# Gate projections in their inputs' banks, attention sums and statistics in the halves of the silu group, and q's projection one half later, in a linear-attention and Mamba kernel

## The chip, the cores and the metric

The kernel runs on one core of one Trainium2 chip. The metric is the device time of a run in microseconds (us), lower is better. The engines are called PE (TensorE), DVE (VectorE), ACT (ScalarE), POOL (GpSimd) and SP (SyncE, which issues all the DMAs here). PSUM is the small memory that PE writes to, in banks of 128 partitions by 512 floats.

## The reference

The input x has shape (8, 512, 48, 48): 8 samples, 512 channels, L = 2304 positions, all in float32. Two layers follow each other, each with a group norm ahead (32 groups of 16 channels) and a residual sum behind it.

```python
# layer 0: causal linear attention, 8 heads of 64
xn = group_norm(x)
q, k = elu(Wq xn) + 1, elu(Wk xn) + 1;  v = Wv xn
S_t = S_(t-1) + k_t v_t^T                       # 64 x 64 per head
out_t = (q_t S_t) / (q_t . cumsum(k)_t + 1e-10)
x = x + out
# layer 1: four Mamba blocks, 128 channels each; each gets the one before added to its input
x_i = group_norm(x)[block i] (+ fused of block i-1)
xp, z = in_proj(x_i);  xs = silu(conv4(xp) + b)  # 256 channels each, 4 causal taps
dt, B, C = x_proj(xs); delta = softplus(dt_proj(dt) + b)
h_t = exp(delta_t A) h_(t-1) + delta_t xs_t B_t  # 16 states per channel
y = (sum_n C_t h_t + xs D) * silu(z);  x_m = out_proj(y)
fused = sigmoid(mean x_i) x_i + sigmoid(mean max(x_i, x_m)) max(x_i, x_m)
x = x + concat(fused)
```

## The kernel before

The whole program is one stream of instructions per engine, in an order that Python code writes out by hand (a manual schedule). Nothing is reordered afterwards: each engine executes its instructions in the order in which they were issued, and waits where one of them needs the result or the buffer of another engine.

**Jobs, slots and halves.** A Mamba block of one sample is cut into six chunks of LC = 384 positions. One chunk is a *job*; there are 8 x 4 x 6 = 192, of two streams (even and odd samples) in turns. A job has 8 *slots*: two halves of the channels by four groups of states. A slot has four scans, so each job has 32 (`scan`, L830, one DVE instruction of 128 x 385). For every scan ACT computes a *decay* (`decay`, L819, an exp into a PSUM bank). DVE makes most of the scan's other input for the next slot at the top of each slot (`product`, L809), POOL the rest of it (`last_product`, L798). POOL multiplies the results with C (`weigh`, L846), PE adds them up in the bank `yp` (`gather`, L853, two slots later), and DVE multiplies by silu(z) (`gated`, L865). `finale` then projects the output (`project`, L871, PE) and takes the maximum (L882, DVE).

All other work is put between the scans. A slot is two *halves*: `beside(2k)` is called after the product and ahead of the first two scans of slot k, `beside(2k + 1)` ahead of the last two. So a job has 16 halves; below they are numbered 0 to 15 within the job that is being scanned, half 0 being its first. Everything else is written as Python generators (tasks) that yield `(when, banks)`: they go on when `when` is due, which is a number of halves since their last stage ("1"), a half (an int), or a half and a gap (a pair), and when so many PSUM banks are free. Attention chunks are kept in the list `heads`, other work in `tasks`; in each half the stages of heads that need no bank are issued first, then tasks and heads in order.

**Banks.** Six PSUM banks, in the list `spare`, are shared by the decays and by every other task. `take` takes the first free one, and `free` puts it back at the end as soon as its last reader has been issued; whoever takes it next waits on the chip for that reader. `ahead(n)` issues decays until n of them are ready or no bank is free: DEPTH = 3 after every scan, DEPTH + 2 before the silu and softplus groups.

**Preparing a job** (`prepare`) is done while the job before it is scanned. The convolutions are matmuls with scaled weights (`conv`, L635), `gate` (L646) is z's projection. Then comes the silu group on ACT (L670 to L675: a table load, four silus; the next decay loads the exp table again), x's projection (L681), a copy to `dbc` (L686), dt's projection (L694), the softplus group (L705, again with a table load ahead and one behind), and the transfers of delta, B and C by SP. In most jobs the silu group is issued in half 14 and the softplus group in half 2. ACT's work on the residual stream (`pass_on`: fu L596, xi L597, xb L601 or L607) is issued in half 2 too, ahead of it.

**Attention** (`chunk`) goes by chunks of 384 positions and 128 channels (two heads), 192 in all. `times[m]` is the half at which chunk m starts; in the steady state it is 3 within the job, so that its stage `at(j)` is issued in half 3 + j of that job or of the next one. The stages: q's projection (`project(0)`, L288, four k-tiles), its features (`feature`: exp L300 and relu L301 on ACT, then min and add on DVE, L345), the same for k (L353) and v (L359), running sums of k (L364, L374), transposes (L381), denominators and products of k and v in one bank called `both` (L393, L398), their sums into S (L401 to L410, DVE), the reciprocal spread over the head (`rdb` L414, transposed into `rb`, L418), the scaled q (L423, DVE), scores (L431), mask (L436), output (L445, L449), residual and statistics (L452, L454). After a block's last chunk `group_norm` computes the norm of layer 1 in five stages (L169 to L195). `statistics` reads the next samples in 24 pieces each for layer 0's norm (L242).

Of the kernel before, what the change touches and what calls it, by code (L numbers as in the profile page):

```python
# [16 lines left out]
P = 128  # L17
# [32 lines left out]
def attention_then_mamba_kernel(  # L50
# [111 lines left out]
    def group_norm(stats, n, name, bufs):  # L162
# [3 lines left out]
        yield "1", 1  # L166
# [5 lines left out]
        yield "1", 0  # L172
# [11 lines left out]
        yield "0", 1  # L184
        var_ps = bank()
        nc.tensor.matmul(var_ps[:, 0:n], grp, gm[:, 2, :], start=True, stop=True)
        yield "1", 0
# [4 lines left out]
        yield "1", 0  # L192
# [16 lines left out]
    def statistics(b):  # L209

        xv = x[b].rearrange("(t p) l -> p t l", p=P)
        stats = small.tile([P, 4, NC, 6], F32, tag="stats_a", name=f"stats_a{b}", bufs=1)
# [20 lines left out]
        else:  # L233
            for ct in range(4):
                for c in range(NC):
                    yield "2", 0
                    if (ct, c) == (0, 0):
                        nxt = piece(b, 0)
                    xs = nxt
                    i = ct * NC + c + 1  # L240
                    nxt = piece(b, i) if i < 4 * NC else None
                    nc.vector.bn_stats(stats[:, ct, c, :], xs)  # L242
# [25 lines left out]
    def chunk(m):  # L268
# [54 lines left out]
        yield at(0), 1  # L323
# [17 lines left out]
        yield at(1), 0  # L341
        ex = feature(qp, qb)
        yield at(2), 0
        q = new("q", 2)
        nc.vector.scalar_tensor_tensor(q, ex, 1.0, qp, ALU.min, ALU.add)  # L345
        bank.free()
        yield at(2, 0), 1
        kp, kb = project(1)
        yield at(3), 0
        ex = feature(kp, kb)  # L350
        yield at(4), 0
        k = new("k", 2)
# [15 lines left out]
        if ksum is not None:  # L368
            kept = new("kept")
            nc.scalar.copy(kept[64:128], kc[64:128])  # L370
            save(ksum[:, cols], kept[64:128])
# [17 lines left out]
        yield at(12), 1  # L389
# [9 lines left out]
        yield at(14), 0  # L399
# [11 lines left out]
        bank.free()  # L411
        yield at(15), 0
        rdb = new("rdb", 1, (P, 2 * NT, 64))
        nc.scalar.copy(rdb, rd.unsqueeze(2).to_broadcast([P, 2 * NT, 64]))  # L414
        yield at(16), 1
        rb = bank()[:, 0:LC].rearrange("p (i t) -> p i t", i=NT)
# [4 lines left out]
        yield at(18), 0  # L421
# [34 lines left out]
        if c + 1 == NC:  # L456
            norm = yield from group_norm(stats, 1, f"m{b}_{o}", 8)
            flush()
            done[b, o] = norm
# [156 lines left out]
    class Job:  # L616
# [6 lines left out]
        def prepare(self):  # L623
# [20 lines left out]
            def gate(h):  # L644
                zp = bank()[:, 0:LC]
# [7 lines left out]
                return zp  # L653
# [5 lines left out]
            yield "1", 1  # L659
            xc0 = conv(0)  # L660
            yield "2", 2
            xc1 = conv(1)
            zp0 = gate(0)
            yield "1", 0
# [6 lines left out]
            bank.free()  # L671
            zp1 = gate(1)
            nc.scalar.activation(xs[:, 1, :], xc1, AF.Silu, bias=pv[:, 1:2])
            nc.scalar.activation(sz[0], zp0, AF.Silu)
            nc.scalar.activation(sz[1], zp1, AF.Silu)  # L675
            converting.clear()
            bank.free(3, late=True)
            yield "1", 1
# [513 lines left out]
```

## Time and profile before

| | |
|---|---|
| runs (median, lowest to highest) | 9334.64 us (9323.44 to 9344.09), 3 runs |
| the profiled execution | 9323.3 us, its span 9321.5 us |
| granted TensorE clock | 0.948 |
| busy: DVE, POOL, PE, ACT | 8348.4, 8080.8, 7735.1, 6580.2 us |
| scans L830 | 6144, 5475.1 us, 938 ns each |
| decays L819 | 6144, 3431.3 us, 579 ns each |
| table loads | 382 ahead of L819, 192 each ahead of L670 and L705, 1283 ns each |
| DMA | 1642.84 MB, 176 GB/s |

A row of the profile gives the line in the kernel, the engine, the operation, the tile that it writes and those that it reads, the count, the busy time and the mean of one, then the idle time of the engine just before these instructions and who ended it. In the waits, "A <- B: us, times, longest" means that engine and line A stood idle until B. In the timeline a row has its start and its duration, both in us from the span's start, and in brackets the idle time before it. Rows of like instructions that follow each other on one engine are merged ("x3"); neighbours on DVE and ACT overlap by some 0.08 us, so that two rows can start closer together than one lasts.

### The profile page before, as it was taken

What the parts mean: (1) busy time and instruction counts of PE and PEld (TensorE: products, weight loads), DVE (VectorE), ACT (ScalarE), POOL (GpSimd) and SP (SyncE); (2) the same over time, 40 slices, a digit from 0 to 9 for tenths busy, and PEclk for the clock granted to TensorE, in tenths of its full rate; (3) what the DMA queues carried; (4) which work ended last, traced back from release to release, by engine and by line L of the source; (5) the groups of instructions that cost most, each with busy time, mean ns of one, the idle gap of its engine ahead of it and who ended that gap; (6) DMA issues with size and microseconds to landing.
All of it is one profiled execution on the core that took longest, in us unless ns stands there. A gap on an engine that the chain in (4) does not pass through costs nothing.

```text
span 9321.5 us, 120629 instructions
## 1 busy us (share of the span) xinstructions
PE 7735.1 (83%) x35714; PEld 3673.0 (39%) x35714; DVE 8348.4 (90%) x11640; ACT 6580.2 (71%) x12656; POOL 8080.8 (87%) x5635
## 2 busy tenths in 40 slices
PE   7888888888888888888888888888888888888865
PEld 4444444433344444443343444443333434444321
DVE  3899999999999999999999999999999999999997
ACT  3677777777777777777777777776777777777775
POOL 2788888889988898889998888888998888888998
PEclk9999999999999999999999999999999999999977
DMA  6566666667666666666766666667666666666654
GB/s 189 158 169 173 175 174 168 180 189 198 188 169 176 177 179 172 176 183 189 196 182 178 174 175 173 174 170 194 192 184 182 176 176 172 173 171 175 167 153 129
DMA packets 1002899, 1642.84 MB, mean 176 GB/s; under 512 B 138592, under 2 KB 797312, under 8 KB 1002240
## 3 DMA queue, kind: packets, MB, share of 16 engines
q1 hardware_dynamic: 1002240, 1635.13, 64.1%
q8 instruction: 283, 4.64, 0.2%
q14 instruction: 376, 3.08, 0.1%
HBM read 1309.06 MB, written 325.58 MB: 175 GB/s over the span
## 4 chain that ended last, share of the span: by engine, by line
DVE 39%; ACT 20%; PE 18%; issue 7%; DMA 7%; POOL 6%; SPq 2%; DVEq 0%; POOLq 0%; ACTq 0%
DVE u L830 23%; DVE u L809 8%; PE bank L288 7%; ACT bank L819 6%; PE bank L635 4%; POOL u L846 4%; ACT L819 3%; PE yp L853 3%; PE bank L646 2%; ACT L705 2%; DMA B<-scr 2%; DMA C<-scr 1%; ACT bank L301 1%; ACT delta L705 1%; DVE sm L436 1%
## 5 line engine op out<-in xcount | busy, mean ns | idle before, releaser
L830 DVE TENSOR_TENSOR_SCAN u<-bank,u 128x385 f32<-128x385 f32 (+1 forms) x6144 | 5475.1, 938 | 530.5 <-ACT bank L819 503.2
L846 POOL TENSOR_TENSOR u<-u,C 128x1536 f32<-128x1536 f32 x1536 | 4885.1, 3180 | 219.5 <-DVE u L830 112.6
L819 ACT ACTIVATE bank<-dr,av 128x385 f32<-128x385 f32 (+1 forms) x6144 | 3431.3, 579 | 1556.9 <-DVE u L830 1113.3
L853 PE MATMUL yp<-u,cst 128*64 128x384 f32 x12288 | 2429.9, 514 | 282.7 <-ACT yp L787 146.3
L798 POOL TENSOR_TENSOR u<-B,dxr 128x512 f32<-128x512 f32 x1536 | 1959.9, 1276 | 22.4 <-DMA dxr<-xscr 19.0
L288 PE MATMUL bank<-xn,wq_sb 128*128 128x384 f32 x4608 | 1855.1, 552 | 48.8 <-DVE u L830 31.7
L809 DVE TENSOR_TENSOR u<-B,dxp 128x1024 f32<-128x1024 f32 x1536 | 1834.7, 1195 | 10.7 <-ACT dxp L782 10.7
L853 PEld LDWEIGHTS yp<-u,cst 128*64 128x64 f32 x12288 | 788.3, 139 | 1476.6 <-issue 903.5
L635 PE MATMUL bank<-xi,wk 128*128 128x384 f32 x3072 | 1118.2, 507 | 280.1 <-ACT kl L385 172.7
L288 PEld LDWEIGHTS bank<-xn,wq_sb 128*128 128x128 f32 x4608 | 929.1, 212 | 862.9 <-issue 215.1
L635 PEld LDWEIGHTS bank<-xi,wk 128*128 128x128 f32 x3072 | 563.7, 193 | 862.2 <-ACT kl L385 254.1
L844 POOL COPY state<-u 128x4 f32<-128x4 f32 x1280 | 243.8, 190 | 740.6 <-DVE u L830 738.0
L300 ACT ACTIVATE ex<-bank,bqkv_sb 128x384 f32<-128x384 f32 x384 | 221.3, 576 | 561.6 <-PE bank L288 539.2
L787 ACT ACTIVATE yp<-xs,pv 128x384 f32<-128x384 f32 x384 | 223.4, 582 | 405.7 <-DVE yz L865 405.7
L819 ACT ACT_TABLE_LOAD x382 | 490.1, 1283 | 6.7
L746 POOL TENSOR_TENSOR delta<-delta,xs 128x384 f32<-128x384 f32 x384 | 385.8, 1005 | 95.5 <-DMA dscr<-delta 84.3
L418 PE MATMUL bank<-cst,rdb 128*128 128x128 f32 x576 | 112.7, 310 | 426.1 <-DVE u L830 334.7
L694 PE MATMUL bank<-dbc,wd 9*128 9x384 f32 x768 | 316.3, 524 | 65.1 <-ACT dbc L686 29.0
L646 PE MATMUL bank<-xi,wi 128*128 128x384 f32 x768 | 297.8, 500 | 59.8 <-ACT xs L670 59.8
L871 PE MATMUL bank<-yz,wo 128*128 128x384 f32 x768 | 297.6, 509 | 34.1 <-DVE yz L865 19.4
L449 PE MATMUL bank<-sm,v 128*64 128x128 f32 x2304 | 257.2, 301 | 42.4 <-DVE u L830 40.6
L418 PEld LDWEIGHTS bank<-cst,rdb 128*128 128x128 f32 x576 | 66.8, 153 | 558.9 <-ACT xb L601 272.5
(109 smaller groups left out, 7860.3 us busy)
## 6 DMA issues: line engine op xcount, KB each, us to landing
B<-scr SPq DMA_DIRECT2D x1536, 192.0 KB
C<-scr SPq DMA_DIRECT2D x1536, 192.0 KB
xn<-xn SPq DMA_DIRECT2D x192, 768.0 KB
dr<-dscr SPq DMA_DIRECT2D x768, 192.0 KB
dxr<-xscr SPq DMA_DIRECT2D x768, 192.0 KB
dscr<-delta SPq DMA_DIRECT2D x192, 384.0 KB
xscr<-delta SPq DMA_DIRECT2D x192, 384.0 KB
xn<-in_x SPq DMA_DIRECT2D x48, 768.0 KB
```

Of the source, the lines that this page charges most:

```text
L288: nc.tensor.matmul(ps, wq_sb[:, kt, j * 512 + o * P : j * 512 + (o + 1) * P], xn[:, kt, :], start=(kt == 0), stop=(kt == 3),)
L635: nc.tensor.matmul(xc, wk[:, k, h * P : (h + 1) * P], xi[:, c0 + k : c0 + k + LC], start=(k == 0), stop=(k == 3),)
L646: nc.tensor.matmul(zp, wi[:, 256 + h * P : 256 + (h + 1) * P], xi[:, c0 + 3 : c0 + 3 + LC], start=True, stop=True,)
L694: nc.tensor.matmul(vp, wd[32:41, h * P : (h + 1) * P], dbc[32:41, :], start=True, stop=True)
L746: nc.gpsimd.tensor_tensor(delta[:, h, :], delta[:, h, :], xs[:, h, :], ALU.mult)
L798: nc.gpsimd.tensor_tensor(u[:, :, :, 1 + LC - TAIL :], self.B[s % 4][:, :, cols].unsqueeze(2).to_broadcast(shape), self.dxr[s // 4][:, :, ...
L809: nc.vector.tensor_mul(u[:, :, :, 1 : 1 + LC - TAIL], self.B[s % 4][:, :, cols].unsqueeze(2).to_broadcast(shape), self.dxp.unsqueeze(1).to ...
L819: nc.scalar.activation(dA[:, cols], self.dr[h][:, g, cols], AF.Exp, scale=self.w[6][:, 2 * h + g, q + j : q + j + 1],)
L830: nc.vector.tensor_tensor_scan(u[:, j, g, cols], dA[:, cols], u[:, j, g, cols], 0.0, ALU.mult, ALU.add,)
L846: nc.gpsimd.tensor_tensor(h, h, self.C[s % 4].unsqueeze(2).to_broadcast([P, NG, 2, LC]), ALU.mult)
L853: nc.tensor.matmul(self.yp[g * 64 : g * 64 + 64, 0:LC], pair_sum, u[:, j, g, 1:], start=False, stop=(s % 4 == 3 and j == NG - 1), skip_gro ...
L871: nc.tensor.matmul(self.xm[:, 0:LC], self.w[2][:, h, :], self.yz[:, h, :], start=(h == 0), stop=(h == 1),)
```

## The change

- `prepare`: the stages of the convolutions and of the silu group get fixed halves, 12, 14 and 15. `gate` no longer takes banks: z's two projections are written into the banks of the two convolutions, each after the silu that reads it. x's projection is issued in the same half as the silu group.
- `chunk`: q's projection with the fetch of the next chunk and the load of `before` moves from `at(0)` to `at(1)`, that is from half 3 to half 4, where the output's projection (L871) is issued ahead of it. q's features move to `at(2)`, and q's min and add to `at(3)`, after k's projection. Denominators and products move from `at(12)` to `at(11)` (half 14), their sums from `at(14)` to `at(13)` (half 0), `rdb` to half 1, `rb` to half 2, the scaled q to half 3. `rb` is written into `both`, which is freed only after it. `kept` shares the buffer of `before`.
- `statistics`: for samples 2 to 7 one piece is loaded per job, two halves ahead, and its statistics are taken in half 15 (even samples) or 0 (odd ones), over 24 jobs; before it was one piece every two halves.
- `group_norm`: the five stages for layer 1 get halves of their own, 13, 14, 0, 1 and 2.

```diff
--- before.py
+++ after.py
@@ -159,17 +159,17 @@
             _, o, i = stores.pop(0)
             nc.sync.dma_start(out=o, in_=i)
 
-    def group_norm(stats, n, name, bufs):
+    def group_norm(stats, n, name, bufs, places=("1", "1", "0", "1", "1")):
 
 
         bank = Banks()
-        yield "1", 1
+        yield places[0], 1
         mv = small.tile([P, n, 2], F32, tag=f"mv{n}", name=f"mv_{name}", bufs=1)
         for ct in range(n):
             nc.vector.bn_aggr(mv[:, ct, :], stats[:, ct].rearrange("p c s -> p (c s)"))
         mean_ps = bank()
         nc.tensor.matmul(mean_ps[:, 0:n], grp, mv[:, :, 0], start=True, stop=True)
-        yield "1", 0
+        yield places[1], 0
         gm = small.tile([P, 3, n], F32, tag=f"gm{n}", name=f"gm_{name}", bufs=1)
         nc.vector.tensor_copy(gm[:, 0, :], mean_ps[:, 0:n])
         nc.vector.tensor_sub(gm[:, 1, :], mv[:, :, 0], mean_ps[:, 0:n])
@@ -181,15 +181,15 @@
         else:
             nc.vector.tensor_mul(gm[:, 2, :], gm[:, 1, :], gm[:, 1, :])
             nc.vector.tensor_add(gm[:, 2, :], gm[:, 2, :], mv[:, :, 1])
-        yield "0", 1
+        yield places[2], 1
         var_ps = bank()
         nc.tensor.matmul(var_ps[:, 0:n], grp, gm[:, 2, :], start=True, stop=True)
-        yield "1", 0
+        yield places[3], 0
         nc.vector.tensor_scalar_add(gm[:, 2, :], var_ps[:, 0:n], 1e-5)
         bank.free()
         norm = small.tile([P, 3, n], F32, tag=f"norm{n}", name=f"norm_{name}", bufs=bufs)
         nc.gpsimd.tensor_tensor(norm[:, 0, :], gm[:, 2, :], power[:, 0:n], ALU.pow)
-        yield "1", 0
+        yield places[4], 0
         for i, factor in ((0, -1.0), (1, float(L))):
             for ct in range(n):
                 nc.vector.tensor_scalar(
@@ -209,7 +209,7 @@
     def statistics(b):
 
         xv = x[b].rearrange("(t p) l -> p t l", p=P)
-        stats = small.tile([P, 4, NC, 6], F32, tag="stats_a", name=f"stats_a{b}", bufs=1)
+        stats = small.tile([P, 4, NC, 6], F32, tag="stats_a", name=f"stats_a{b}", bufs=2)
         if b == 0:
 
             xs = []
@@ -231,15 +231,13 @@
             for o in range(1, 4):
                 load_projections(o)
         else:
-            for ct in range(4):
-                for c in range(NC):
-                    yield "2", 0
-                    if (ct, c) == (0, 0):
-                        nxt = piece(b, 0)
-                    xs = nxt
-                    i = ct * NC + c + 1
-                    nxt = piece(b, i) if i < 4 * NC else None
-                    nc.vector.bn_stats(stats[:, ct, c, :], xs)
+            when = begins[b] + b % 2
+            for i in range(4 * NC):
+                yield (when - 2, 1) if b > 1 else "1", 0
+                xs = piece(b, i)
+                yield (when, 1) if b > 1 else "1", 0
+                nc.vector.bn_stats(stats[:, i // NC, i % NC, :], xs)
+                when += PERIOD
         norms[b] = yield from group_norm(stats, 4, f"a{b}", 2)
 
     def piece(b, i):
@@ -320,7 +318,7 @@
             save(xns[b].rearrange("(t p) l -> p t l", p=P)[:, :, cols], xn)
         while read[0] < m - 1:
             yield "1w", 0
-        yield at(0), 1
+        yield at(1), 1
         if o:
             xn = fetched.pop(m)
         if c == 0:
@@ -338,18 +336,16 @@
             for h in heads_of:
                 nc.sync.dma_start(out=before[h], in_=passes[b, o - 1][2][:, cols])
         qp, qb = project(0)
-        yield at(1), 0
+        yield at(2), 0
         ex = feature(qp, qb)
-        yield at(2), 0
-        q = new("q", 2)
-        nc.vector.scalar_tensor_tensor(q, ex, 1.0, qp, ALU.min, ALU.add)
-        bank.free()
         yield at(2, 0), 1
         kp, kb = project(1)
         yield at(3), 0
+        q, k = new("q", 2), new("k", 2)
+        nc.vector.scalar_tensor_tensor(q, ex, 1.0, qp, ALU.min, ALU.add)
+        bank.free()
         ex = feature(kp, kb)
         yield at(4), 0
-        k = new("k", 2)
         nc.vector.scalar_tensor_tensor(k, ex, 1.0, kp, ALU.min, ALU.add)
         bank.free()
         yield at(4, 0), 1
@@ -366,7 +362,7 @@
             nc.tensor.matmul(kc, ident, before, start=False, stop=True)
         yield at(8), 0
         if ksum is not None:
-            kept = new("kept")
+            kept = new("before")
             nc.scalar.copy(kept[64:128], kc[64:128])
             save(ksum[:, cols], kept[64:128])
         yield at(9), 0
@@ -386,7 +382,7 @@
         nc.scalar.copy(v, turned[1])
         bank.free(2)
 
-        yield at(12), 1
+        yield at(11), 1
         both = bank()
         den = both[:, 0 : 2 * NT]
         for i in range(NT):
@@ -396,7 +392,7 @@
         for i in range(more):
             for h in heads_of:
                 nc.tensor.matmul(ds[h, i, :], kl[:, i, h], v[:, i, h], start=True, stop=True)
-        yield at(14), 0
+        yield at(13), 0
         rd = small.tile([P, 2 * NT], F32, tag="rd", name=f"rd_{n}", bufs=1)
         nc.vector.tensor_scalar_add(rd, den, 1e-10)
         nc.vector.reciprocal(rd, rd)
@@ -408,17 +404,17 @@
                 nc.vector.tensor_copy(S[:, place[1], :], ds[:, 0, :])
             else:
                 nc.vector.tensor_add(S[:, place[i + 1], :], S[:, place[i], :], ds[:, i, :])
-        bank.free()
-        yield at(15), 0
+        yield at(14), 0
         rdb = new("rdb", 1, (P, 2 * NT, 64))
         nc.scalar.copy(rdb, rd.unsqueeze(2).to_broadcast([P, 2 * NT, 64]))
-        yield at(16), 1
-        rb = bank()[:, 0:LC].rearrange("p (i t) -> p i t", i=NT)
+        yield at(15), 0
+
+        rb = both[:, 0:LC].rearrange("p (i t) -> p i t", i=NT)
         for i in range(NT):
             nc.tensor.transpose(
                 rb[:, i, :], rdb[:, 2 * i : 2 * i + 2, :].rearrange("p e d -> p (e d)"), ident
             )
-        yield at(18), 0
+        yield at(16), 0
 
         nc.vector.tensor_mul(q, q, rb.rearrange("p i t -> p (i t)"))
         bank.free()
@@ -454,7 +450,9 @@
         nc.vector.bn_stats(stats[:, 0, c, :], xr)
         save(x1s[b][tile_rows, cols], xr)
         if c + 1 == NC:
-            norm = yield from group_norm(stats, 1, f"m{b}_{o}", 8)
+            norm = yield from group_norm(
+                stats, 1, f"m{b}_{o}", 8, [(times[m] + j, 1) for j in (26, 27, 29, 30, 31)]
+            )
             flush()
             done[b, o] = norm
 
@@ -641,8 +639,7 @@
                     )
                 return xc
 
-            def gate(h):
-                zp = bank()[:, 0:LC]
+            def gate(h, zp):
                 nc.tensor.matmul(
                     zp,
                     wi[:, 256 + h * P : 256 + (h + 1) * P],
@@ -650,32 +647,31 @@
                     start=True,
                     stop=True,
                 )
-                return zp
 
 
             while converting or not st.scaled:
                 yield "1w", 0
             converting.append(n)
-            yield "1", 1
+            first = 2 * self.start
+            yield (first - 20, 1), 1
             xc0 = conv(0)
-            yield "2", 2
+            yield (first - 18, 2), 1
             xc1 = conv(1)
-            zp0 = gate(0)
-            yield "1", 0
+            yield (first - 17, 1), 0
             xs = self.xs = mpool.tile([P, 2, LC], F32, tag="xs", name=f"xs_{n}")
             sz = self.sz = [
                 mpool.tile([P, LC], F32, tag="sz", name=f"sz_{n}_{h}", bufs=5) for h in range(2)
             ]
             ahead(DEPTH + 2)
             nc.scalar.activation(xs[:, 0, :], xc0, AF.Silu, bias=pv[:, 0:1])
-            bank.free()
-            zp1 = gate(1)
+
+            gate(0, xc0)
             nc.scalar.activation(xs[:, 1, :], xc1, AF.Silu, bias=pv[:, 1:2])
-            nc.scalar.activation(sz[0], zp0, AF.Silu)
-            nc.scalar.activation(sz[1], zp1, AF.Silu)
+            gate(1, xc1)
+            nc.scalar.activation(sz[0], xc0, AF.Silu)
+            nc.scalar.activation(sz[1], xc1, AF.Silu)
             converting.clear()
-            bank.free(3, late=True)
-            yield "1", 1
+            bank.free(2, late=True)
             dps = bank()
             for h in range(2):
                 nc.tensor.matmul(
@@ -744,7 +740,6 @@
             for h in range(2):
                 yield "1", 0
                 nc.gpsimd.tensor_tensor(delta[:, h, :], delta[:, h, :], xs[:, h, :], ALU.mult)
-            first = 2 * self.start
             yield "2", 0
             xsrc = spread("xscr")
             spreading.clear()
@@ -962,12 +957,17 @@
         if job.c == NC - 1:
             yield from job.stream.pass_on()
 
+
     begun, put, counted = 0, 0, list(range(1, B))
+    begins = {}
+    for b in counted:
+        first = times[parts.index((b, 0, 0))]
+        begins[b] = (first - 20) // PERIOD * PERIOD - 4 * NC * PERIOD - 1 if b > 1 else first - 64
 
     def begin(latest):
 
         nonlocal begun, put
-        while counted and times[parts.index((counted[0], 0, 0))] - 64 <= half_no[0]:
+        while counted and begins[counted[0]] - 4 <= half_no[0]:
             tasks.append(Task(statistics(counted.pop(0))))
         while put < len(parts) and times[put] - 6 <= half_no[0]:
             put += 1
```

## The prediction

> **What bounds the kernel now.** I read the busy shares on the page first, then the waits, then one pass of 16 halves in the timeline, engine by engine.
>
> ```profile
> PE 7735.1 (83%) x35714; PEld 3673.0 (39%) x35714; DVE 8348.4 (90%) x11640; ACT 6580.2 (71%) x12656; POOL 8080.8 (87%) x5635
> ```
>
> VectorE (DVE) is busy 8348.4 of 9321.5 us. The change removes no VectorE instruction, so its idle 973 us are what can be won, and new idle time there is what can be lost. The table of waits says who ends that idle time (total us, times, longest):
>
> ```profile
> DVE u L830 <- ACT bank L819: 503.2, 194, 4.7
> PE bank L418 <- DVE u L830: 334.7, 149, 2.8
> DVE q L345 <- ACT bank L301: 141.5, 63, 6.6
> DVE k L353 <- ACT bank L301: 70.8, 144, 2.3
> ```
>
> The scan waits for its decay (ScalarE, L819) once in each of the 192 jobs, 2.6 us on average. The other two VectorE waits are for q's and k's features. The timeline shows where the first lies (start, us, engine and line), in the job whose half 0 starts at 4972.03:
>
> ```profile
> 5010.54 1.19 DVE L809 TENSOR_TENSOR u<-B,dxp 128x1024 f32<-128x1024 f32 x1
> 5011.65 2.64 DVE L830 TENSOR_TENSOR_SCAN u<-bank,u 128x384 f32<-128x384 f32 x3
> 5017.47 0.96 DVE L830 TENSOR_TENSOR_SCAN u<-bank,u 128x384 f32<-128x384 f32 x1 [3.17 <-ACT bank L819]
> 5018.34 1.20 DVE L809 TENSOR_TENSOR u<-B,dxp 128x1024 f32<-128x1024 f32 x1
> ```
> ```profile
> 5011.04 1.10 ACT L819 ACTIVATE bank<-dr,av 128x384 f32<-128x384 f32 x2
> 5012.16 1.28 ACT L670 ACT_TABLE_LOAD   x1
> 5015.05 0.49 ACT L675 ACTIVATE sz<-bank 128x384 f32<-128x384 f32 x1 [0.15 <-PE bank L646]
> 5015.56 1.28 ACT L819 ACT_TABLE_LOAD   x1
> 5016.85 1.09 ACT L819 ACTIVATE bank<-dr,av 128x384 f32<-128x384 f32 x2
> ```
>
> Half 14 starts at 5010.54. The silu group (two table loads, four silus) holds ScalarE from 5012.16 to 5016.84, 4.68 us. Three decays were ahead; VectorE runs their three scans and stands 3.17 us. The next product (L809), 1.11 us of ready work, comes after the stalled scan in program order. Of these waits 159 lie in half 15 and 31 in half 0, the latter in jobs whose weights came late, so that their silu group was already issued in half 15; these are 2.4 us.
>
> The softplus group of half 2 is as heavy (1.28 + 0.87 + 1.28), yet costs nothing now:
>
> ```profile
> 4978.67 0.56 ACT L819 ACTIVATE bank<-dr,av 128x384 f32<-128x384 f32 x1
> 4979.25 1.28 ACT L705 ACT_TABLE_LOAD   x1
> 4981.43 1.28 ACT L819 ACT_TABLE_LOAD   x1
> ```
> ```profile
> 4978.57 3.49 DVE L830 TENSOR_TENSOR_SCAN u<-bank,u 128x384 f32<-128x384 f32 x4
> 4981.98 1.19 DVE L809 TENSOR_TENSOR u<-B,dxp 128x1024 f32<-128x1024 f32 x1
> ```
>
> Four scans run on without a gap, because the decay at 4978.67, a fourth one ahead, found a free bank. Lastly TensorE around half 4, which starts at 4981.98:
>
> ```profile
> 4979.66 0.52 PE L418 MATMUL bank<-cst,rdb 128*128 128x128 f32 x3 [2.32 <-DVE u L830]
> 4980.42 2.85 PE L288 MATMUL bank<-xn,wq_sb 128*128 128x384 f32 x8 [0.24 <-DVE u L830]
> 4983.10 1.50 PE L871 MATMUL bank<-yz,wo 128*128 128x384 f32 x4
> 4986.50 1.51 PE L853 MATMUL yp<-u,cst 128*64 128x384 f32 x8 [1.90 <-ACT yp L787]
> 4987.94 2.85 PE L288 MATMUL bank<-xn,wq_sb 128*128 128x384 f32 x8
> ```
>
> q's projection (first L288) fills TensorE while it would otherwise wait for yz; then the output's (L871), a gather (L853), k's projection.
>
> **What the skill says.** The Trainium skill, "ScalarE: Activation LUTs", section What ACT_TABLE_LOAD costs, gives about 1283 ns for a load plus 1380 ns of drain. The trace has the 1283 ns, but the work before ended 0.02 us ahead of the load at 4979.25: no drain shows, and I price a switch at 1.28 us. "PSUM — Partial Sum Buffer", section Terms, says that TensorE writing and another engine reading one bank at once is an error. So a gate projection into its input's bank has to wait for the silu that reads it; the trace has this wait already for the second gate (L646 after xs L670: 196.5 us, TensorE and its loads together). "Perfetto Trace Analysis", section Optimization Strategy, says that a gap that keeps repeating on the engine to be saturated can mean too few buffers. The 3.17 us gap agrees: three of the six shared banks hold convolutions and gate, so only three decays fit.
>
> **The change, part by part**, in us per job; "pitch" is from start to start.
>
> *Silu group one half later, sums and statistics moved.* At half 15 three decays are again ahead: the gates free one bank, but `both` is now taken in half 14 and holds it. From the end of the last scan of half 14, ScalarE needs a decay 0.6, the group 4.68 and a decay 0.58: 5.86. VectorE has two scans 1.74, the product 1.11, the sums (0.13 + 0.19 + three of 0.21, with gaps 0.95), 0.4 as the mean of a bn_stats (0.54, in three jobs of four), a scan 0.87: 5.07. Leaves 0.8. The late-weight jobs bear it out from the other side: 2.4 measured with the group in half 15, less 1.35 of moved work, is 1.05. To that comes the gates' turn-taking: the first gate waits for the first silu (0.58), runs 0.7, and sz follows; the second the same. At least 0.5. If TensorE also has den, S's products and a gather ahead (convolution 2.85 + 1.35 + 1.5 from about 5010.8: done 5016.6, the first silu at 5015.95), 1.15. I take a stall of 1.8, from 1.3 to 2.2. Against about 3.0 in 118 ordinary jobs that is −1.2, −142; the late-weight ones give −0.3 each, −9; the 30 with a norm at the end (now 1.3) nothing. Sum **−150**, from −260 to −60.
>
> *`both` held through rb.* This removes rb's own bank and its 2.32 us wait on TensorE. That is worth nothing directly, since q's projection has to wait for L871 anyway. But the bank is held from half 14 to half 3, where before it was free from 1 to 3. In half 2 it stands with two softplus inputs and three decays: six, and the fourth decay does not fit. Then from the start of half 2, ScalarE needs 0.1 + 0.57 (third decay, whose bank the last scan has just freed), fu 0.51, xi 0.51, mostly xb 0.6, table 1.29, softplus 0.89, table 1.30, decay 0.59: 6.36 with xb, 5.76 without. VectorE has product 1.11, two scans 1.71, the moved q product (L423) 0.46, a scan 0.87: 4.15. A new stall of 2.2 or 1.6, less the 0.35 that some jobs now lose in half 4. About +1.8 in 150 jobs: **+270**, from +60 (if fu and xi get out of the way) to +330.
>
> *q one half later.* With X the start of half 4: yz ends at X+1.66, L871 0.96 later as now, q 2.85, gather 1.44, k 2.85: k's projection ends at X+9.76 where now it ends at X+8.81. Exp and Relu add 1.03: k can be read at X+10.8. VectorE comes to L353 after half 4 (3.29), half 5 without L423 and L345 (3.10 − 0.91), half 6 with q's (1.11 + 0.46 + 1.71): X+8.76. The stall is 2.05 against 0.60 in this job: +1.45 in 177 jobs (those with their chunk at the usual place), **+257**, from +90 to +400. q's own is read after X+5.47+1.03 = 6.5, and VectorE is at 6.6: its 141.5 us shrink to about 20, **−121**.
>
> *The rest.* The norm's waits (L188, 29.4 us, for L186) get a half of their own in places: −15, from −29 to +30. The statistics' loads keep two halves of lead, at most +15.4 again (L242 for its DMA). The transfers of q's stage (fetch, `before`) leave SP one half later and are used by half 10 or in the next job; SP's B and C rows stand next to them, and 96 KB more beside 1635 MB over the span cost nothing while there are 6 halves of cover. The sharing of `kept` with `before` waits for a store 7 halves old. GpSimd (87%) gets no new work, and its waits follow VectorE's.
>
> Sum: −150 + 270 + 257 − 121 − 15 = **+241** on the span of 9321.5. The profiled run took 9323.3, so 9564 beside it; the median of the runs is 9334.6, 11 more, so 9575 beside the median, which I give.
>
> **Rivals.** (1) Faster: the stall behind silu is covered and neither new wait bites. One mechanism, k's features: if TensorE has L871 and q done early enough (k's projection done by X+7.7) and a fourth bank is there for softplus, the sum is −150 − 121 − 15 = −286: 9050. It decides below 1.5 us per job for both waits together (286 / 190). For it: stalls behind ScalarE are the largest idle item. Against: L871 can't start before yz, and 2.85 + 1.44 + 2.85 behind it are in order. (2) Only one of the two waits bites: −286 + 270 or + 257, about −20: 9315, no change within the measurement (0.2%, some 19 us, is about what a measurement of this kernel can tell). (3) Worse: gates and held banks put whole stages off by halves (needs of two banks in halves 1, 6 and 12 are met exactly), and the silu stall stays: 400 to 600 more, 9800. (4) The change doesn't do what it says: if `both` were full later than half 14, silu could have four decays ahead, and 0.87 × 150 = 130 come off my sum: 9455; I count it to mine.
>
> **Numbers.** My case 0.60 (own range 9430 to 9730), rival 1 0.15, rival 2 0.18 (a third on each side), rival 3 0.07. Faster 0.15 + 0.06 = 0.21, same 0.07, slower 0.72. The range of 8 in 10 leaves out most of rivals 1 and 3: 9190 to 9730.
>
> **What would show it.** Right: a new idle of 1.5 to 2.3 us before the fourth scan of half 3, ended by L819; L353's waits for L301 near 340 us in place of 70.8; L345's under 40; L418's wait for L830 gone; the scan's stall of half 15 gone and one of 1.3 to 2.2 in half 0; VectorE's busy time as before. Wrong: four scans without a gap after L705's table load, or k's second L288 ending before X+8.8, or L830's wait for L819 under 400 us.

## The result: 7.0% slower, and the profile after

The changed kernel takes 9982.33 us (median of 4 runs, 9981.9 to 9982.99), against 9329.04 us of the kernel before in the same runs: ratio 1.0698, 95% interval 1.0679 to 1.0716. The profiled execution has a span of 9980.4 us, 658.9 more than before, and a granted TensorE clock of 0.887 (0.948 before). Lines of the kernel have moved a little: the scan is L825 now, the decay L814, the output's projection L866, the projections of q, k and v L286, Exp and Relu L298 and L299, q's and k's min and add L345 and L349; each experiment moves them a little again, so that the scan is L823 to L830 below.

From the page, first the busy times, then the rows of the scan and of the output's projection, each before and after (busy us, mean ns of one; then the idle time before it and its releaser):

```profile
PE 8143.0 (82%) x35714; PEld 3880.4 (39%) x35714; DVE 8381.2 (84%) x11640; ACT 6601.9 (66%) x12656; POOL 8093.0 (81%) x5635
L830 DVE TENSOR_TENSOR_SCAN u<-bank,u 128x385 f32<-128x385 f32 (+1 forms) x6144 | 5475.1, 938 | 530.5 <-ACT bank L819 503.2
L825 DVE TENSOR_TENSOR_SCAN u<-bank,u 128x385 f32<-128x385 f32 (+1 forms) x6144 | 5497.0, 941 | 666.5 <-ACT bank L814 660.9
L871 PE MATMUL bank<-yz,wo 128*128 128x384 f32 x768 | 297.6, 509 | 34.1 <-DVE yz L865 19.4
L866 PE MATMUL bank<-yz,wo 128*128 128x384 f32 x768 | 518.9, 771 | 879.1 <-DVE yz L860 751.9
```

VectorE has the same work (8381.2 us, 33 more); the loss is idle time. TensorE has the same matmuls, but the output's projection takes 771 ns for each of its matmuls where it took 509. The table of waits:

```profile
DVE u L825 <- ACT bank L814: 660.9, 364, 4.3
DVE q L345 <- ACT bank L299: 365.7, 188, 5.6
DVE k L349 <- ACT bank L299: 351.7, 189, 2.0
PE bank L866 <- DVE yz L860: 751.9, 187, 4.8
```

The scan now waits for its decay 364 times, twice per job, and q's and k's features are late in nearly every job, not in 63 and 144 of 192. TensorE's wait for yz is new. One job shows how these follow each other. VectorE, from half 3 to half 7:

```profile
3285.26 0.53 DVE L419 TENSOR_TENSOR q<-q,bank 128x384 f32<-128x384 f32 x1
3285.71 0.95 DVE L825 TENSOR_TENSOR_SCAN u<-bank,u 128x385 f32<-128x385 f32 x1
3289.00 0.96 DVE L825 TENSOR_TENSOR_SCAN u<-bank,u 128x385 f32<-128x385 f32 x1 [2.34 <-ACT bank L814]
...
3290.98 0.55 DVE L860 TENSOR_TENSOR yz<-yp,sz 128x384 f32<-128x384 f32 x1
...
3298.64 0.55 DVE L345 SCALAR_TENSOR_TENSOR q<-ex,bank 128x384 f32<-128x384 f32 x1 [1.97 <-ACT bank L299]
...
3302.86 0.55 DVE L349 SCALAR_TENSOR_TENSOR k<-ex,bank 128x384 f32<-128x384 f32 x1 [1.95 <-ACT bank L299]
```

TensorE over the same stretch:

```profile
3285.85 1.15 PE L866 MATMUL bank<-yz,wo 128*128 128x384 f32 x2 [0.36 <-DVE q L419]
3291.59 1.65 PE L866 MATMUL bank<-yz,wo 128*128 128x384 f32 x2 [4.59 <-DVE yz L860]
3293.03 4.52 PE L286 MATMUL bank<-xn,wq_sb 128*128 128x384 f32 x8
3297.48 1.51 PE L848 MATMUL yp<-u,cst 128*64 128x384 f32 x8
3298.92 2.85 PE L286 MATMUL bank<-xn,wq_sb 128*128 128x384 f32 x8
```

ScalarE, with the softplus group, then q's Exp:

```profile
3284.90 1.28 ACT L701 ACT_TABLE_LOAD   x1
3286.20 0.87 ACT L701 ACTIVATE delta<-bank 128x384 f32<-128x384 f32 x2
3287.08 1.28 ACT L814 ACT_TABLE_LOAD   x1
3288.38 1.09 ACT L814 ACTIVATE bank<-dr,av 128x385 f32<-128x385 f32 x2
3297.59 0.58 ACT L298 ACTIVATE ex<-bank,bqkv_sb 128x384 f32<-128x384 f32 x1 [3.78 <-PE bank L286]
```

The scan of half 3 stands 2.34 us, because its decay is behind the softplus group. So half 4 and yz come later, and TensorE, with nothing but the output's projection at the head of its queue, is idle for 4.59 us. Then the output's second half takes 1.65 us for two matmuls and q's projection 4.52 us for eight; k's, a little later, takes 2.85 for eight of the same shape. The stretches say why (length; busy us and count of PE, PEld, DVE, ACT and POOL; granted TensorE clock; DMA share and GB/s):

```profile
3285.00:3291.00 6.00, 1.63 (x4) 0.50 (x2) 3.66 (x6) 5.53 (x9) 4.10 (x5) 0.78 1.03 286
3291.00:3298.00 7.00, 6.41 (x14) 3.39 (x16) 5.65 (x9) 2.65 (x6) 6.92 (x7) 0.60 0.86 256
3298.00:3302.00 4.00, 4.00 (x20) 1.89 (x16) 2.27 (x3) 1.81 (x5) 4.00 (x3) 1.00 0.06 23
```

The granted clock is 0.60 on average while the output and q are projected, and 1.00 for k. The Trainium skill, "TensorE: Matmul & The Clock Gate", section HAM oscillation, gives the rule that TensorE should have no idle gaps above about 3.4 us, since it comes back at half clock. In this job the 4.59 us gap and the 0.60 behind it agree; other runs do not bear the length out (see e9_bank_back_busy_pe).

### The profile page after: what moved, and what is told of

It reads as the page before. It is cut to its first block, busy times and chain, and to the rows that moved or that the text cites. A ratio compares the mean times of both kernels' runs of the same rounds, so it can differ in the third digit from the quotient of the medians.

```text
span 9980.4 us, 120128 instructions
## 1 busy us (share of the span) xinstructions
PE 8143.0 (82%) x35714; PEld 3880.4 (39%) x35714; DVE 8381.2 (84%) x11640; ACT 6601.9 (66%) x12656; POOL 8093.0 (81%) x5635
## 4 chain that ended last, share of the span: by engine, by line
DVE 31%; PE 29%; ACT 25%; issue 7%; DMA 4%; POOL 3%; SPq 1%; DVEq 0%; POOLq 0%; ACTq 0%
DVE u L825 18%; PE bank L286 13%; DVE u L804 8%; ACT bank L814 8%; ACT L814 5%; PE yp L848 4%; PE bank L633 4%; PE bank L866 3%; PE bank L643 3%; DMA dxr<-xscr 3%; ACT L701 2%; ACT L666 2%; POOL u L841 2%; ACT delta L701 1%; DVE yz L860 1%
## 5 line engine op out<-in xcount | busy, mean ns | idle before, releaser
L825 DVE TENSOR_TENSOR_SCAN u<-bank,u 128x385 f32<-128x385 f32 (+1 forms) x6144 | 5497.0, 941 | 666.5 <-ACT bank L814 660.9
L814 ACT ACTIVATE bank<-dr,av 128x385 f32<-128x385 f32 (+1 forms) x6144 | 3403.9, 579 | 1167.4 <-DVE u L825 988.1
L848 PE MATMUL yp<-u,cst 128*64 128x384 f32 x12288 | 2612.6, 534 | 99.0 <-POOL u L841 80.9
L286 PE MATMUL bank<-xn,wq_sb 128*128 128x384 f32 x4608 | 1928.9, 570 | 4.9 <-POOL xn L310 2.4
L633 PE MATMUL bank<-xi,wk 128*128 128x384 f32 x3072 | 1200.1, 537 | 443.5 <-DVE u L825 413.9
L286 PEld LDWEIGHTS bank<-xn,wq_sb 128*128 128x128 f32 x4608 | 1020.1, 228 | 946.3 <-issue 464.9
L848 PEld LDWEIGHTS yp<-u,cst 128*64 128x64 f32 x12288 | 838.5, 143 | 1218.2 <-issue 920.1
L866 PE MATMUL bank<-yz,wo 128*128 128x384 f32 x768 | 518.9, 771 | 879.1 <-DVE yz L860 751.9
L633 PEld LDWEIGHTS bank<-xi,wk 128*128 128x128 f32 x3072 | 591.9, 203 | 1019.1 <-DVE u L825 564.6
L298 ACT ACTIVATE ex<-bank,bqkv_sb 128x384 f32<-128x384 f32 x384 | 222.9, 581 | 1134.6 <-PE bank L286 1134.6
L782 ACT ACTIVATE yp<-xs,pv 128x384 f32<-128x384 f32 x384 | 224.6, 585 | 751.5 <-DVE yz L860 751.4
L866 PEld LDWEIGHTS bank<-yz,wo 128*128 128x128 f32 x768 | 169.5, 275 | 1215.1 <-DVE yz L860 885.2
L345 DVE SCALAR_TENSOR_TENSOR q<-ex,bank 128x384 f32<-128x384 f32 x192 | 106.3, 554 | 365.7 <-ACT bank L299 365.7
L349 DVE SCALAR_TENSOR_TENSOR k<-ex,bank 128x384 f32<-128x384 f32 x192 | 106.4, 554 | 351.7 <-ACT bank L299 351.7
```

Of the source, the lines that this page charges most:

```text
L286: nc.tensor.matmul(ps, wq_sb[:, kt, j * 512 + o * P : j * 512 + (o + 1) * P], xn[:, kt, :], start=(kt == 0), stop=(kt == 3),)
L633: nc.tensor.matmul(xc, wk[:, k, h * P : (h + 1) * P], xi[:, c0 + k : c0 + k + LC], start=(k == 0), stop=(k == 3),)
L814: nc.scalar.activation(dA[:, cols], self.dr[h][:, g, cols], AF.Exp, scale=self.w[6][:, 2 * h + g, q + j : q + j + 1],)
L825: nc.vector.tensor_tensor_scan(u[:, j, g, cols], dA[:, cols], u[:, j, g, cols], 0.0, ALU.mult, ALU.add,)
L848: nc.tensor.matmul(self.yp[g * 64 : g * 64 + 64, 0:LC], pair_sum, u[:, j, g, 1:], start=False, stop=(s % 4 == 3 and j == NG - 1), skip_gro ...
L866: nc.tensor.matmul(self.xm[:, 0:LC], self.w[2][:, h, :], self.yz[:, h, :], start=(h == 0), stop=(h == 1),)
```

## The experiments

A and B in the expectations are the theories that three waits add up, or that the held bank is the root of all of it; C is that the clock makes the excess over the forecast.

**Two of the change's parts, undone one by one and together.** e1_q_back:

```diff
-        yield at(1), 1
+        yield at(0), 1
...
         qp, qb = project(0)
+        yield at(1), 0
+        ex = feature(qp, qb)
         yield at(2), 0
-        ex = feature(qp, qb)
+        q = new("q", 2)
+        nc.vector.scalar_tensor_tensor(q, ex, 1.0, qp, ALU.min, ALU.add)
+        bank.free()
         yield at(2, 0), 1
         kp, kb = project(1)
         yield at(3), 0
-        q, k = new("q", 2), new("k", 2)
-        nc.vector.scalar_tensor_tensor(q, ex, 1.0, qp, ALU.min, ALU.add)
-        bank.free()
         ex = feature(kp, kb)
         yield at(4), 0
+        k = new("k", 2)
...
```

> The changed kernel with one part undone: q's projection, features, min and add back in halves 3, 4 and 5, k's after them, as before the change; rb still goes into the held bank, silu group, sums and statistics stay moved. Theory A (three separate waits on VectorE: the place of q costs 365.7 + 351.7 - 141.5 - 70.8 = +505, the held bank about +319, the silu part gives -183): 9982 - 505 = about 9480; the waits of q and k for L299 fall to 200 us in sum or less, the idle time in half 3 (1.79 us per job) stays. Theory B (the held bank starves every task, and the waits of q and k are its consequence): under 150 us less, 9830 or more. Theory C (TensorE's halved clock alone makes the excess over the forecast): the granted clock goes back to about 0.94 since q again fills the wait for yz, and the time falls by about 345, to 9640.

e2_bank_back:

```diff
                 nc.vector.tensor_add(S[:, place[i + 1], :], S[:, place[i], :], ds[:, i, :])
+        bank.free()
...
-        yield at(15), 0
-        rb = both[:, 0:LC].rearrange("p (i t) -> p i t", i=NT)
+        yield at(16), 1
+        rb = bank()[:, 0:LC].rearrange("p (i t) -> p i t", i=NT)
...
-        yield at(16), 0
+        yield at(18), 0
         nc.vector.tensor_mul(q, q, rb.rearrange("p i t -> p (i t)"))
```

> The changed kernel with the other part undone: the bank of denominators and products is freed after the sums in half 0, rb takes a bank of its own in half 3, the scaled q is in half 5. q's projection stays in half 4. Theory A: the softplus group has a fourth decay ahead again, the idle time in half 3 goes (1.79 us per job), q's and k's waits stay at about 700 us in sum: 9982 - 320 = about 9660. Theory B: most of the 653 us come back, 9450 or less.

e2_bank_back moves one thing more on VectorE: the scaled q goes from half 3, ahead of yz, to half 5, behind it. e4_both_back has both edits.

> The changed kernel with both parts undone: q back in halves 3 to 5, rb in a bank of its own with the scaled q in half 5, the bank of the sums freed in half 0. What stays of the change: gates in their inputs' banks, the silu group one half later, sums in half 0, statistics in halves 15 and 0, the norm's stages, the shared buffer. Theory A: 9982 - 505 - 320 = about 9150, 2% under the kernel before: the silu part alone is worth -183. Theory B and C have no reason for a gain over the kernel before: 9330 or more. A risk in both: the scaled q in half 5 comes after q's features again.

Measured: e1_q_back 9419.62 us (ratio to the kernel before 1.0095, interval 1.0075 to 1.0115), e2_bank_back 9499.65 (1.0181, 1.0160 to 1.0201), e4_both_back 9291.17 (0.9955, 0.9938 to 0.9972). As a table:

| | bank held through rb | bank freed after the sums |
|---|---|---|
| q in half 4 | 9982.3 | 9499.7 |
| q back in half 3 | 9419.6 | 9291.2 |

q's place costs 208 us with the bank freed and 563 with it held; the bank costs 128 with q early and 483 with q late. The two do not add: together they cost 691, of which 691 − 208 − 128 = 355 are there only when both are. Theory B falls with e1_q_back (it expected 9830 or more), and so does C's 9640 there, while A's 9480 is 60 off; e2_bank_back came 160 under A's figure and 50 above B's. What is left of A is that each of its waits exists, but they do not add. e2_bank_back's waits, and its row of the scan:

```profile
DVE k L349 <- ACT bank L299: 354.3, 190, 2.0
DVE u L825 <- ACT bank L814: 338.5, 191, 3.9
DVE q L345 <- ACT bank L299: 135.2, 158, 5.6
L825 DVE TENSOR_TENSOR_SCAN u<-bank,u 128x385 f32<-128x385 f32 (+1 forms) x6144 | 5461.5, 939 | 448.5 <-ACT bank L814 338.5
```

Freeing the bank takes away the second stall per job (364 waits to 191). It does not bring the scans to 338.5 us of idle time, though, but to 448.5: 107 us lie in half 4 (5.5 in the changed kernel, 30 before), and the profile puts most of them down to "issue" or to GpSimd, though they end within 0.12 us of a decay's end.

230 of q's 365.7 us go as well, although q's projection is at the same place. Most of this is not TensorE's doing. In the 180 jobs with their chunk at the usual place q's projection ends 5.6 us after yz on average, where it ended 6.0 us after it, while VectorE comes to q's features 6.2 us after yz in place of 5.2: the scaled q and the waits of half 4 now lie between the two. How much of q's wait hangs on the stall in half 3 is therefore read from e7_rb_early_q_late below, which leaves the scaled q ahead of yz.

e4_both_back was expected at 9150; it gains 0.5%, not 2%. The scans' idle time is 452.1 us there, 78 less than before and not 183 less, because of the same waits in half 4 (110 us). And q's and k's waits are 33.7 and 231.0 us, 264.7 together, where 212.3 were expected to come back: k's features are late, which A had left out.

**TensorE kept busy.** e3_busy_pe adds work to the changed kernel and takes nothing away:

```diff
+        yield at(0), 1
+        spin = bank()[:, 0:LC]
+        for _ in range(6):
+            nc.tensor.matmul(spin, ident, cst[:, 0:LC], start=True, stop=True)
+        bank.free()
         yield at(1), 1
```

> The changed kernel with work added: in half 3 of each chunk six products of the identity with constants (128 x 128 by 128 x 384, some 4.3 us of TensorE at the full clock, 830 us in all) go into a free bank that nobody reads, just where TensorE waits for yz ahead of the output's and q's projection. Theory C (the q term was missed because TensorE stands 5 to 6 us before yz, its clock is halved, and output's and q's projection then take 1.7 and 4.5 us where 0.96 and 2.85 were counted): more work makes it faster; q's projection has a median under 3.2 us, q's wait for L299 falls from 365.7 to under 80, the time by 250 to 350, to about 9680. Rival D (order alone: q stands behind the output's projection, whatever the clock): q's wait stays over 300, the time is 9970 or more.

Measured: 9710.69 us (1.0407, 1.0386 to 1.0428), 272 less than the changed kernel, with the clock at 0.942. Its waits:

```profile
DVE u L830 <- ACT bank L819: 692.0, 373, 6.4
DVE k L354 <- ACT bank L299: 327.6, 190, 2.4
DVE q L350 <- ACT bank L299: 70.4, 59, 7.4
```

q's wait falls from 365.7 to 70.4 and the median of q's projection, first matmul to last, from 4.42 to 2.74 us; the stalls of half 3 and of k stay. 192 x 6 products that nobody reads make the kernel 2.7% faster: theory C holds for q's wait, D falls. (The added products also take a bank for a moment; the scan's wait is 31 us longer for it or for another reason, so that the gain does not come from there.) e9_bank_back_busy_pe puts the same six products into e2_bank_back, to see whether the clock is what couples the two parts.

> e2_bank_back with the added six products in half 3 of e3_busy_pe. With the stall of half 3 gone TensorE's wait for yz is short already. If the clock is what couples the two losses, the added work is now worth less than the 272 us that it gave the changed kernel: q's wait falls from 135 to under 80, the time to 9400 to 9480. If the clock is independent of the stall in half 3: another 250 less, 9250.

Measured: 9464.82 us (1.0149, 1.0131 to 1.0168), in the range that was expected if the clock couples the two. The added work is worth 35 us here, not 272. TensorE recovers all the same: the granted clock is 0.951 (0.898 in e2_bank_back), and q's projection takes 2.74 us in the median, where it took 4.24. But there was less to win. q's wait was 135.2 us and loses 72, and the maximum behind the output's projection, which now comes after the added products, waits 37 us anew:

```profile
DVE q L350 <- ACT bank L299: 63.5, 54, 9.6
DVE fg L882 <- PE bank L871: 36.7, 34, 2.4
```

With TensorE kept busy, freeing the bank brings 9711 − 9465 = 246 us, where it brought 483 without; with q early it brings 128. Of the 355 us of coupling some 237 are thus q's wait: freeing the bank cuts it by 230 us (365.7 to 135.2) where TensorE is not kept busy, and by 7 (70.4 to 63.5) where it is. Most of the other 118 is k's: with q early k's wait grows by 97 us when the bank is freed (133.6 to 231.0), with q late it does not (351.7, 354.3).

e2_bank_back also shows that a long gap is not needed for a low clock. TensorE's wait for yz is 2.4 us there at the longest, and yet q's projection takes over 3.2 us in 176 of 192 chunks (178 in the changed kernel). One of them:

```profile
3085.91 1.65 PE L866 MATMUL bank<-yz,wo 128*128 128x384 f32 x2 [0.73 <-DVE u L825]
3088.34 1.65 PE L866 MATMUL bank<-yz,wo 128*128 128x384 f32 x2 [0.78 <-DVE yz L860]
3089.78 4.25 PE L286 MATMUL bank<-xn,wq_sb 128*128 128x384 f32 x8
3081.00:3088.00 7.00, 5.68 (x17) 1.84 (x15) 7.00 (x9) 6.94 (x13) 5.67 (x5) 0.61 0.82 199
3088.30:3094.00 5.70, 5.66 (x12) 2.91 (x12) 5.41 (x8) 4.07 (x10) 5.70 (x4) 0.60 0.87 265
```

The granted clock is 0.61 and 0.60 with no gap above 0.8 us. So here the measurement differs from the skill's figure: what brings the clock down in this job stays open, and only that more work on TensorE brings it up again is shown.

**The bank freed earlier.** e7_rb_early_q_late keeps q in half 4 and rb in the held bank, one half earlier:

```diff
-        yield at(14), 0
+        yield at(13, 0), 0
         rdb = new("rdb", 1, (P, 2 * NT, 64))
...
-        yield at(15), 0
+        yield at(14), 0
         rb = both[:, 0:LC].rearrange("p (i t) -> p i t", i=NT)
...
-        yield at(16), 0
+        yield at(15), 0
         nc.vector.tensor_mul(q, q, rb.rearrange("p i t -> p (i t)"))
```

> The changed kernel with rb one half earlier as in e5_rb_early and q's projection left in half 4 as the change put it. If the two losses feed each other (the stall in half 3 lengthens TensorE's wait for yz, the clock halves, q's projection is late), the release of the bank alone brings back about as much as in e2_bank_back: 9450 to 9510, q's wait near 135 us, k's near 350. If they are independent: 9982 less 230, 9750.

Measured: 9558.6 us (1.0247, 1.0227 to 1.0268), 424 less than the changed kernel, near the coupled expectation but 50 above its range: q still waits 215.3 us, k 364.3. The scan's wait is 345.3 us, and the idle time of all scans 386.9: the second stall is gone although rb still uses the held bank. What cost time in half 3 was the fourth decay, not the sharing. q's wait is 150 us shorter than in the changed kernel. VectorE comes to q's features 5.4 us after yz here, nearly as in the changed kernel (5.2), but q's projection ends 5.4 us after yz and not 6.0, and TensorE's wait for yz is 410.6 us, 751.9 there. So the stall in half 3 does make q late, by some 0.6 us per job. e5_rb_early joins this with e1_q_back's edit.

> q's projection back in half 3 as in e1_q_back, rb still in the bank of denominators and products, but one half earlier: the reciprocal is spread in half 0 behind the sums, rb comes in half 1 and the scaled q in half 2, ahead of the softplus group, so that the bank is free when that group asks for a fourth decay. If the held bank costs time only by the missing fourth decay: the 1.79 us idle in half 3 go, about 0.6 come back in half 4 as in e4_both_back, k's wait stays between 134 and 231 us: 9420 less 0.9 to 1.4 times 190, 9150 to 9250, faster than the kernel before. If holding the bank costs in other ways (other tasks late, TensorE waiting for banks), it stays at 9400.

Measured: 9302.26 us (0.9971, 0.9959 to 0.9982). The stall in half 3 is gone, but the expectation was missed by 50: k's wait is 255.7 us, above the 134 to 231 assumed. With rb in the shared bank the release of the bank brings 424 us with q late and 117 with q early, so the coupling (306) is there without the scaled q behind yz too.

**The gates alone.** e6_gates_only is the kernel before with one edit, so that two banks are held ahead of the silus in place of three:

```diff
-            zp0 = gate(0)
...
-            bank.free()
-            zp1 = gate(1)
+            gate(0, xc0)
             nc.scalar.activation(xs[:, 1, :], xc1, AF.Silu, bias=pv[:, 1:2])
+            gate(1, xc1)
...
```

> The kernel before with the gates alone changed: z's projections go into the banks of the convolutions, nothing moves otherwise. In half 14 only two banks are then held, so four decays fit ahead of the silu group in place of three: 0.87 us more cover, less 0.3 to 0.7 for the silus that wait for their gate in turn. Theory A: the scan's wait for L819 falls from 503 to 400 to 470 us, the time by 30 to 100, to about 9265. Rival: the turn-taking costs as much as the decay gives (another 0.87 or more on ScalarE): 9330 or slower.

Measured: 9337.73 us, ratio 1.0005 (0.9997 to 1.0014), no change. The wait that the profile puts down to the decay falls from 503.2 to 62.9 us, but most of the rest is the same wait under another name. The row of the scan, then one job:

```profile
L827 DVE TENSOR_TENSOR_SCAN u<-bank,u 128x385 f32<-128x385 f32 (+1 forms) x6144 | 5459.6, 938 | 396.2 <-issue 188.8
3246.28 3.50 DVE L827 TENSOR_TENSOR_SCAN u<-bank,u 128x385 f32<-128x385 f32 x4
3253.20 0.96 DVE L827 TENSOR_TENSOR_SCAN u<-bank,u 128x384 f32<-128x384 f32 x1 [2.31 <-issue]
3250.08 0.49 ACT L671 ACTIVATE sz<-bank 128x384 f32<-128x384 f32 x1 [0.53 <-PE bank L645]
3251.24 1.28 ACT L816 ACT_TABLE_LOAD   x1
3252.53 1.09 ACT L816 ACTIVATE bank<-dr,av 128x384 f32<-128x384 f32 x2
```

Four scans run in place of three, as expected. Then the first scan of half 0 stands 2.31 us and starts 0.09 us after its decay has ended (the first of the two at 3252.53, 0.58 us long). "issue" says only that the profile shows no releaser; the silu group holds this scan too, and it is longer by the gates' turns (0.53 us for L645). Of the 396.2 us, 388 end within 0.12 us of a decay's end. So the scans lose 134 us of idle time, near what theory A forecast, but the time does not fall: 68.2 us come up for the denominators (L401 for PE L398), and k's wait goes from 70.8 to 132.7. By halves, 2.3 us per job leave half 15, 1.5 come in half 0, 0.4 in half 1 and 0.3 in half 7. TensorE waits 269.1 us for the silus ahead of the gates, 59.8 before, and the denominators stand behind the gates in its queue; that this makes them late fits, but was not tested.

**A version that beats both.** In e5_rb_early, k's projection stands behind a gather (L848) that waits for ACT's skip copy (L782; 370.2 us over all gathers, TensorE and its loads together). e8_k_early issues it ahead; against e5_rb_early:

```diff
         ex = feature(qp, qb)
+        yield at(1, 0), 1
+        kp, kb = project(1)
         yield at(2), 0
         q = new("q", 2)
...
-        yield at(2, 0), 1
-        kp, kb = project(1)
         yield at(3), 0
```

> e5_rb_early with one further step: k's projection is issued in half 4, right behind q's and the output's, ahead of the gather that waits for the skip copy L782; k's features and L351 stay in halves 6 and 7. In e5_rb_early k's projection ended 2 us after VectorE needed it (L351 waits 255.7 us for L299). If that wait is a matter of TensorE's order alone, it falls under 60 us and the time to about 9110 (9302 - 195), 2.3% under the kernel before. If TensorE is full in halves 3 to 6, the gather that is now behind only hands the wait on (yz L860 for L848, or q's L343): 9250 or more.

Measured: 9106.41 us (9095.94 to 9110.3), ratio 0.976 (0.9747 to 0.9774), as expected if TensorE's order alone made k late. k's wait is 11.9 us; VectorE's longest are now:

```profile
DVE u L825 <- ACT bank L814: 344.7, 195, 6.3
DVE xr L448 <- PE bank L445: 55.8, 33, 7.5
DVE q L345 <- ACT bank L299: 43.5, 113, 3.1
```

So the silu part of the change, with the bank free before softplus asks for it and with q projected in half 3 and k in half 4 ahead of the gather, is worth 2.4% over the kernel before. Of these 218 us some 196 came with the last step, which is no part of the change; what it would bring to the kernel before alone was not run (k's wait is 70.8 us there).

## Why the prediction was right on three steps and wrong on one

| step | predicted | measured |
|---|---|---|
| silu group, sums and statistics | −150 | −165 (338.5 − 503.2; the 338.5 from e2_bank_back) |
| held bank, fourth decay missing | +270 | +322 (660.9 − 338.5) |
| k's features | +257 | +281 (351.7 − 70.8) |
| q's features | −121 | **+224** (365.7 − 141.5) |
| the rest | −15 | about 0 (norm's wait −27, VectorE busy +33) |
| sum | +241 | +666 (the spans differ by 658.9) |

(The two upper rows count the waits named for the decay. All idle time of the scans, from 530.5 to 666.5, is +136, where the two rows give +157.)

The direction, slower, was forecast at 0.72, and the waits lie in the halves that were named. The 9982 us lie outside the range, and the step that failed is one: q's chain, "q 2.85" with "L871 0.96 later as now", which put the end of q's projection 3.8 us behind yz (6.0 on average, as measured) and made q's wait shrink by 121. L866 ends 1.7 us after yz in the job shown, not 0.96, and q's projection takes 4.42 in the median, not 2.85: together 2.3 us, enough to turn 0.1 us of spare time into a wait of 1.9 in the mean. The prediction had no term for TensorE's granted clock. Its 2.85 was read from one row of one job, and the kernel before had the warning in it, one job later:

```profile
5025.99 0.56 PE L418 MATMUL bank<-cst,rdb 128*128 128x128 f32 x3 [2.33 <-DVE u L830]
5026.74 4.32 PE L288 MATMUL bank<-xn,wq_sb 128*128 128x384 f32 x8 [0.20 <-DVE u L830]
```

Measured from first to last matmul, 132 of its 192 projections of q took over 3.2 us (mean 3.97), while k's and v's took 2.85 in the median. The mean over all of them would have shown it.

That k's row is so close is in part luck. k's projection ends 10.2 us after yz on average, where 8.1 were forecast, but VectorE, held up by q's wait, also comes to k's features later, 9.35 us after yz and not 7.1: two errors of over 2 us that cancel. Where q's chain is near its forecast, in e3_busy_pe, k's wait is up by 257 as well, so the step itself, k behind q and the output, was right.

The sum itself was the second weakness. I treated the stall in half 3 and the place of q as two separate terms, while the first feeds the second: a stall on VectorE is idle time on TensorE, whose next instruction waits for VectorE. e7_rb_early_q_late shows 150 us of q's wait that go with the stall; the table of four shows the coupling of the two parts, 355, and e3_busy_pe what more work on TensorE brings, 272. With TensorE busy the forecast's terms land closer: in e3_busy_pe the scan's wait is up by 189, k's by 257 and q's down by 71, 375 in all, where −150 + 270 + 257 − 121 = 256 were forecast, and the time is up by 381.

Two slips in the working change nothing in this: 130 off 9575 is 9445, not 9455, and the three shares of "slower" add to 0.73.

The rivals: "faster" needed both waits short, and neither was; "only one bites" fell with the waits as they are; "worse" came nearest in size (9800) but with the wrong reason: it kept the silu stall, which did shrink. That rb's own wait on TensorE (334.7 us) is worth nothing directly agrees with two runs: e4_both_back, where rb has a bank of its own again, takes 9291, e5_rb_early, where it has none, 9302.

## What to carry to other kernels

When work is moved away from where an engine would otherwise wait, ask what fills that wait afterwards; here TensorE also ran what came behind an empty wait at a lower granted clock. Take a duration from all its instances at the place that it moves to, and sort them, before one row is put into a chain. A buffer that is held longer costs where the number of free ones sets how far another engine runs ahead: count the free buffers in each stage, not the waits for the buffer itself. Before a wait counts as gone, add up the idle time at its line under every name, "issue" included.

## What was not expected of the hardware

TensorE work that nobody reads made the kernel 272 us faster, with 192 x 6 products (2304 matmul rows in the trace) put into a wait of up to 4.8 us. And eight matmuls of one shape took 4.52 us at a granted clock around 0.60 and 2.85 us at 1.00, within 6 us of each other. In e2_bank_back the clock was as low without any gap above 0.8 us before it.
